# Moving the product for the maxima, the background slots and the first and last steps of a fused perceiver layer

## The chip, the core and the metric

One core of one Trainium2 chip runs the whole program. The time is device microseconds of one launch; a kernel's figure is the median of its runs. Engines are named as in the profile: PE (TensorE), DVE (VectorE), ACT (ScalarE), POOL (GpSimd), SP (the queue that issues most transfers).

## What is computed

x is (4, 256, 256), the context is (4, 4096, 256), all in float32. The reference applies three residual layers in turn:

```
x = x + cross_attention(layernorm(x), context)      # 8 heads of 64; keys and values of x and of the context joined: 4352 keys
x = routed(x)     # layernorm; a small network ranks the 256 tokens of a batch: the top 64 go through
                  # self-attention, the other 192 through a state-space scan (512 channels, 16 states)
x = x + experts(layernorm(x))    # router picks 2 of 8 experts per token: down(silu(gate(x)) * up(x))
```

## The kernel before

**Main loop.** The cross-attention is cut into 16 groups G (4 batches of 4 head pairs) and each group into 8 steps s, so n = 8G+s runs over N = 128 steps and two more. A step takes 32 queries of two heads against all keys. On PE it computes `scores(n)` into one PSUM area `su` (L1384, L1391). DVE copies `su` to SBUF and takes each row's maximum (`copy_max`, L1403, and the small `mq`, L1410). `stat(n)` is a product on PE that brings together the four partial maxima of a query (L1415, its result lies in `su` too); DVE reduces it to `nb` (L1420). ACT applies exponentials one step later (`exps(n-1)`, L1431), and DVE transposes the two heads (`turn(n-1, 0)`, `turn(n-1, 1)`, L1440). `scores(n+1)` overwrites `su`, so it waits for `nb`.

**Pieces.** The rest of PE's time in a step is filled with pieces of other work. In steps s=2, 3, 4 they are `v_chunk` (values of 512 context rows, L1368), nine per group; in s=6, 7, 0 `k_chunk` (keys for the next group, L1330, eight) and `k_self` (queries and own keys, L1341); in s=1 and 5, the value steps, four pieces of `values` (probabilities times values, L1449). `load_ctx` (L1235) brings each chunk's context tile on SP, in four buffers. In the first group step 1 has no piece, and in the last group steps 0, 6 and 7 have none.

**Sums.** At s=0, `sums(G-1)` forms reciprocals of the softmax sums; `spread` writes them to DRAM, `fetch` (L1486, on ACT's queue, at s=1) reads them back broadcast as `rs`, and `normalize` (L1502) multiplies each half of the output `ao` by them. `project` (L1506) and `add` put a finished batch into `x_sb`.

**Background.** Everything else of a batch runs as generators beside the main loop: `routed(b)` with router, self-attention, `ssm_front`, `ssm_scan`, `ssm_back`, then `sortable` and, for batch 2, `dispatch`, which sorts tokens of three batches by expert. Each generator yields (delay, share): it goes on no earlier than `now` plus delay, and only in a slot that has so much room left. `now` is a hand-written clock that the loop advances by estimated PE times; `slot(budget)` stands at fixed places of a step and lets each waiting generator take one stretch. So the order of instructions on every engine is fixed when the program is written, and each engine works its queue in order. In a scan stretch DVE runs one scan (L743) and POOL multiplies by `cb` (L749) and adds twice to `y` (L751); after two scans ACT makes new exponentials `da` (L731) and POOL new products `db` (L736). Each batch has 32 scans.

The fourth batch's background, the experts of the sorted tokens (19 blocks) and the dense experts of the last batch follow behind the main loop, once `dispatch` has set `ready`.

## Time and profile before

| | us |
|---|---|
| median of 3 runs | 1528.92 (1523.39 to 1531.32) |
| the profiled execution | 1526.89 |
| its span, first to last instruction | 1525.1 |
| main loop, from the first scores to the last ones' end | 24.9 to about 1242 |
| PE, DVE, ACT, POOL busy | 1444.4, 1061.7, 758.6, 404.5 |

A group's row gives an engine and a source line, the tiles it writes and reads, the count, the busy time and the mean in ns of one, then the engine's idle time ahead of these instructions and what ended it. A row of the waits gives who waited for whom: us in total, times, longest. A row in order of time gives start, duration, engine, line, and in brackets the idle time before it with its releaser. PE counts as busy while products overlap, so gaps show where it had nothing to do, not how fast it was.

### The profile page before, as it was taken

The page shows a single profiled execution, that of the slowest core. Times are in us where ns is not written, and L with a number is a line of the kernel's source. Part 1 is how long each engine was busy: PE and PEld are TensorE (multiplying, and loading weights), DVE is VectorE, ACT ScalarE, POOL GpSimd, SP SyncE. Part 2 cuts the span into 40 slices and gives each one's busy share as a digit, 9 for nine tenths or more (in the row PEclk, how much of TensorE's full clock was granted, in tenths as well). Part 3 has the DMA queues.
Part 4 walks back from the last instruction along what each step waited for, and adds up shares of the span by engine and source line. Part 5 has one row for each costly group of instructions (what it writes and reads, how often), then busy time and mean ns, then how long its engine had stood idle before and what let it go on. Part 6 is the DMA issues. An engine that isn't in the chain of part 4 may idle for free.

```text
span 1525.1 us, 35283 instructions
## 1 busy us (share of the span) xinstructions
PE 1444.4 (95%) x14630; PEld 1021.4 (67%) x14630; DVE 1061.7 (70%) x1824; ACT 758.6 (50%) x1484; POOL 404.5 (27%) x467
## 2 busy tenths in 40 slices
PE   7999999999999999999999999999998968898999
PEld 3747566677666566676757575767575657888887
DVE  1656665656698986666889956666989663699353
ACT  3444454454665645455766544556655522553311
POOL 1000000000078860000598800001989101111020
PEclk9999999999999999999999999999999979999999
DMA  6555534424445343425454444352543333787661
GB/s 230 156 148 150 162 117 155 156 88 138 136 132 173 122 136 128 157 78 154 145 151 145 147 142 132 105 164 87 191 138 107 105 125 114 218 274 232 222 198 53
DMA packets 160352, 225.42 MB, mean 148 GB/s; under 512 B 15520, under 2 KB 78752, under 8 KB 160192
## 3 DMA queue, kind: packets, MB, share of 16 engines
q1 hardware_dynamic: 149632, 208.96, 43.5%
q10 hardware_dynamic: 9072, 10.13, 2.0%
q0 software_dynamic: 1488, 4.07, 0.9%
q8 instruction: 116, 1.90, 0.5%
q14 instruction: 44, 0.36, 0.1%
HBM read 218.66 MB, written 4.46 MB: 146 GB/s over the span
## 4 chain that ended last, share of the span: by engine, by line
PE 60%; DVE 20%; POOL 9%; issue 5%; DMA 3%; ACT 2%; SPq 0%; ACTq 0%; DVEq 0%; POOLq 0%
PE psv L1368 10%; PE su L1384 10%; PE po L1449 10%; PE psk L1330 9%; DVE sp L1403 6%; DVE db L743 4%; POOL y L751 3%; POOL db L749 3%; POOL db L736 3%; DVE pt L1440 3%; PE su L1391 2%; PE pde L1906 2%; PE pg L1893 2%; PE pu L1893 2%; DVE db L839 2%
## 5 line engine op out<-in xcount | busy, mean ns | idle before, releaser
L1403 DVE TENSOR_SCALAR_CACHE_REDUCE sp<-su 128x1088 f32<-128x1088 f32 x256 | 318.8, 1282 | 186.8 <-PE su L1391 186.8
L1440 DVE STREAM_TRANSPOSE pt<-sp 128x1088 f32<-128x1088 f32 x256 | 327.5, 1293 | 30.6 <-PE po L1449 26.6
L1431 ACT ACTIVATE sp<-sp,nb 128x1088 f32<-128x1088 f32 x256 | 305.1, 1195 | 15.7 <-DVE nb L1420 13.8
L1449 PE MATMUL po<-pt,v 128*64 128x128 f32 x4352 | 261.0, 278 | 2.1 <-DVE pt L1440 1.3
L1384 PE MATMUL su<-kt,qh 64*32 64x512 f32 x4096 | 256.3, 610 | 4.5 <-DVE nb L1420 4.0
L1330 PE MATMUL psk<-ctx,wk 128*128 128x512 f32 x512 | 245.9, 614 | 11.7 <-DMA ctx<-in_ctxT 8.0
L1368 PE MATMUL psv<-wv,ctx 128*128 128x128 f32 x2048 | 252.3, 280 | 0.0
L1449 PEld LDWEIGHTS po<-pt,v 128*64 128x64 f32 x4352 | 242.4, 139 | 11.9 <-issue 6.3
L1368 PEld LDWEIGHTS psv<-wv,ctx 128*128 128x128 f32 x2048 | 237.7, 193 | 11.1 <-issue 8.9
L1330 PEld LDWEIGHTS psk<-ctx,wk 128*128 128x128 f32 x512 | 91.7, 192 | 100.3 <-issue 92.6
L1318 ACT COPY kt<-psk 128x512 f32<-128x512 f32 x128 | 74.6, 585 | 155.8 <-PE psk L1330 155.5
L1384 PEld LDWEIGHTS su<-kt,qh 64*32 64x32 f32 x4096 | 63.1, 108 | 124.0 <-issue 95.5
L1372 ACT COPY v<-psv 128x512 f32<-128x512 f32 x144 | 79.4, 558 | 134.1 <-PE psv L1368 132.8
L751 POOL TENSOR_TENSOR y<-y,db 128x192 f32<-128x192 f32 x192 | 139.7, 728 | 15.0
L743 DVE TENSOR_TENSOR_SCAN db<-da,db 128x384 f32<-128x384 f32 x96 | 126.4, 1317 | 11.4 <-POOL y L751 0.5
L749 POOL TENSOR_TENSOR db<-db,cb 128x384 f32<-128x384 f32 x96 | 108.1, 1126 | 43.6 <-DVE da L741 43.6
L395 POOL TENSOR_TENSOR kbd<-qk,hmask 128x512 f32<-128x512 f32 x8 | 8.6, 1096 | 403.1 <-ACT qk L385 403.1
L731 ACT ACTIVATE da<-delta,A_log_sb 128x192 f32<-128x192 f32 x192 | 75.4, 447 | 51.0 <-DVE da L741 31.5
L736 POOL TENSOR_TENSOR db<-bb,xc 128x384 f32<-128x384 f32 x96 | 99.5, 1059 | 0.2
L1391 PEld LDWEIGHTS su<-kx,qh 128*32 128x32 f32 x1024 | 20.2, 108 | 109.4 <-issue 109.4
L1415 PEld LDWEIGHTS su<-mq,same 128*128 128x128 f32 x256 | 40.8, 190 | 66.3 <-DVE mq L1410 46.9
L1496 ACT COPY ao<-po 128x128 f32<-128x128 f32 x32 | 8.4, 264 | 139.5 <-PE po L1449 139.5
(297 smaller groups left out, 1569.3 us busy)
## 6 DMA issues: line engine op xcount, KB each, us to landing
ctx<-in_ctxT SPq DMA_DIRECT2D x256, 512.0 KB
gateT<-in_gateT SPq DMA_DIRECT2D x27, 512.0 KB
upT<-in_upT SPq DMA_DIRECT2D x27, 512.0 KB
downT<-in_downT SPq DMA_DIRECT2D x27, 512.0 KB
bb<-bcd SPq DMA_DIRECT2D x24, 192.0 KB
cb<-bcd SPq DMA_DIRECT2D x24, 192.0 KB
wv<-in_wv SPq DMA_DIRECT2D x32, 128.0 KB
in_w<-in_in_w SPq DMA_DIRECT2D x32, 128.0 KB
```

The source lines that it names most:

```text
L736: nc.gpsimd.tensor_tensor(db, bbs[k], bc(xc[:, m, :], 1, SG), ALU.mult)
L743: nc.vector.tensor_tensor_scan(out=db, data0=da, data1=db, initial=0.0, op0=ALU.mult, op1=ALU.add,)
L749: nc.gpsimd.tensor_tensor(db, db, cbs[k], ALU.mult)
L751: nc.gpsimd.tensor_tensor(y[:, m, :], y[:, m, :], db[:, s, :], ALU.add)
L1330: nc.tensor.matmul(ps, wqk[G][:, 0, c, :], ct[:, c, :], start=(c == 0), stop=(c == KD - 1),)
L1368: nc.tensor.matmul(ps[:, i * P : (i + 1) * P], lhsT, wv[G][:, w, c, :], start=(c == 0), stop=(c == KD - 1),)
L1372: nc.scalar.copy(v.rearrange("p k d -> p (k d)"), ps[:, : n * P])
L1384: nc.tensor.matmul(su[q * 32 : (q + 1) * 32, SC[j] + lo : SC[j] + lo + 512], qT[r, s * 32 : (s + 1) * 32], kt[r, q, lo : lo + 512], start= ...
L1403: nc.vector.tensor_scalar(out=sps[n][j], in0=su[:, SU[j] : SU[j] + QK], scalar1=1.0, scalar2=None, op0=ALU.mult, op1=ALU.max, accum_out=nm ...
L1431: nc.scalar.activation(sps[n][j], sps[n][j], AF.Exp, bias=nbs[n][:, j : j + 1], accum_out=lss[b][:, hp, s, j : j + 1],)
L1440: nc.vector.transpose(pts[m, j][:, i, :], sps[n][j])
L1449: nc.tensor.matmul(pos[m][j * HD : (j + 1) * HD, :], vts[m // 2, k // 4][:, k % 4, j * HD : (j + 1) * HD], pts[m, j][:, :, kk * 32 : (kk + ...
```

## The change

In steps that aren't value steps, `stat` moves from ahead of the third piece into its middle (`mid`); in value steps it moves behind the third piece, and the first `normalize` follows it. A slot is added in value steps ahead of the first piece; in scan stretches some slots shrink to one scan, and a scan may follow after 1.9 instead of 2.2. Parts of `dispatch` may join in one slot (`fits`), and the last seven steps get larger slots (`more`). The first group's value chunks start in step 1, the last group's in its step 0, in a free key buffer. The late loads start at 70 instead of 15, and group 1's `wself` is loaded in step 6. The last batch's projection is done for three head pairs in step 126 and for the fourth at the end; a projection's two halves share one bank and are added together. In `ssm_back`, both products come ahead of both copies.

```diff
@@ -766,7 +766,7 @@
...
                     else:
-                        yield 2.2, 1.4
+                        yield 1.9, 1.4
@@ -873,6 +873,7 @@
                     ps[:n, q * D : (q + 1) * D], zs[:, m, q * P : q * P + n],
                     ow[m // 2][:, m % 2, :], start=(m == 0), stop=(m == NDT - 1),
                 )
+        for q, n in ((0, P), (1, NBOT - P)):
             nc.scalar.copy(dsort[:n, q, :], ps[:n, q * D : (q + 1) * D])
@@ -909,7 +911,10 @@
...
             yield 3.0, 0
+        if not late:
+            scanning.add(b)
         yield from st["late"] if late else ssm_scan(b, st)
+        scanning.discard(b)
@@ -1107,7 +1112,8 @@
...
-        yield 1.0, 1.25
+        if not fits(1.25):
+            yield 1.0, 1.25
         chosen(sl, slot)
@@ -1135,7 +1142,8 @@
...
         ats = []
         for i, tag in enumerate(("ua", "permT", "dsort")):
-            yield 1.0, 0.7
+            if not fits(0.7):
+                yield 1.0, 0.7
             at = bg.tile([P, 4, P], F32, tag=tag, name="at")
@@ -1173,6 +1181,13 @@
...
+
+    def fits(share):
+
+        if room[0] < share:
+            return False
+        room[0] -= share
+        return True
@@ -1253,13 +1268,14 @@
...
         def load_later():
 
-            yield 15.0, 0
+            yield 70.0, 0
             for b in range(1, B):
                 load_x(b)
                 yield 2.0, 0
             nc.sync.dma_start(out=wo, in_=a["xwo"].rearrange("(c p) m -> p c m", p=P))
             yield 2.0, 0
             yield from load_consts()
+            yield 10.0, 0
             start(routed(0))
@@ -1320,7 +1336,7 @@
...
-        def k_chunk(G, g):
+        def k_chunk(G, g, mid=None):
...
                     ps, wqk[G][:, 0, c, :], ct[:, c, :],
                     start=(c == 0), stop=(c == KD - 1),
                 )
+                if mid and c == 0:
+                    mid()
             keys_out(G, g * (CK // 4), ps)
@@ -1351,15 +1369,23 @@
...
-        def v_chunk(G, g):
+        def v_chunk(G, g, mid=None):
 
             b = G // NHP
             n = 4 if g < NCH else 2
-            v = wk.tile([P, n, P], F32, tag=f"v{n}", name="v", bufs=NCH if g < NCH else 1)
+            if G == NG - 1 and g < 3:
+
+                if g == 0:
+                    vts["first"] = wke.tile([P, 4, SQ], F32, tag="kt", name="vfirst")
+                v = vts["first"][:, g, : n * P].rearrange("p (k d) -> p k d", d=P)
+            else:
+                v = wk.tile([P, n, P], F32, tag=f"v{n}", name="v", bufs=NCH if g < NCH else 1)
             ps = ps_m.tile([P, 512], F32, tag="m", name="psv")
             if g < NCH:
                 ct = load_ctx(b, g)
             for i in range(n):
+                if mid and 2 * i == n - n % 4:
+                    mid()
@@ -1501,32 +1527,28 @@
...
+        def project(b, hps):
+
+            ps = bank("psx")
+            for half in range(2):
+                for hp in hps:
+                    nc.tensor.matmul(
+                        ps[:, half * D : (half + 1) * D],
+                        aos[b, hp][:, half * P : (half + 1) * P], wo[:, hp, :],
+                        start=(hp == hps[0]), stop=(hp == hps[-1]),
+                    )
+            return ps
+
+        def add(b, ps):
+            for half in range(2):
+                xb = x_sb[:, 2 * b + half, :]
+                nc.vector.tensor_tensor(xb, xb, ps[:, half * D : (half + 1) * D], ALU.add)
...
         def finish_batch(b):
 
             yield 1.0, 0.9
-            if b in psx:
-                ps, done_hp = psx[b], NHP - 1
-            else:
-                ps, done_hp = bank("psx"), 0
-                project(b, 0, ps, range(NHP))
-                add(b, 0, ps)
-            project(b, 1, ps, range(done_hp, NHP))
-            add(b, 1, ps)
+            add(b, project(b, range(NHP - 1 if b == B - 1 else 0, NHP)))
             finished.add(b)
@@ -1551,35 +1573,46 @@
...
-                if s % 4 == 1:
+                if G == 0 and s == 1:
+                    pieces = [lambda g=g: v_chunk(G, g) for g in range(2)]
+                elif s % 4 == 1:
                     m, took = n // 4 - 1, 1.95
-                    if m >= 0:
-                        pieces = [
-                            lambda i=i: values(m, i, min(i + 9, NJ)) for i in range(0, NJ, 9)
-                        ]
-                elif 2 <= s <= 4 and G < NG:
                     pieces = [
-                        lambda g=g: v_chunk(G, g) for g in range(3 * s - 6, 3 * s - 3)
+                        lambda i=i: values(m, i, min(i + 9, NJ)) for i in range(0, NJ, 9)
+                    ]
+                elif G < NG and (2 <= s <= 4 or s == 0 and G == NG - 1):
+                    at = {0: (2, 5, 7, 9), NG - 1: (3, 6, 8, 9)}.get(G, (0, 3, 6, 9))
+                    if s == 0:
+                        at = (0, at[0])
+                    else:
+                        at = at[s - 2 : s]
+                    pieces = [
+                        lambda mid=None, g=g: v_chunk(G, g, mid) for g in range(*at)
                     ]
                 elif G + 1 < NG:
                     if s == 0:
                         wqk[G + 1] = load_qk(G + 1)
+                    if s == (6 if G == 0 else 0):
                         wself[G + 1] = load_self(G + 1)
                     pieces = {
-                        0: [lambda g=g: k_chunk(G + 1, g) for g in range(3)],
-                        6: [lambda g=g: k_chunk(G + 1, g) for g in range(3, 6)],
+                        0: [lambda mid=None, g=g: k_chunk(G + 1, g, mid) for g in range(3)],
+                        6: [lambda mid=None, g=g: k_chunk(G + 1, g, mid) for g in range(3, 6)],
                         7: [lambda: k_self(G + 1)]
-                        + [lambda g=g: k_chunk(G + 1, g) for g in range(6, 8)],
+                        + [lambda mid=None, g=g: k_chunk(G + 1, g, mid) for g in range(6, 8)],
                     }[s]
...
-                def piece(i):
+                def piece(i, **mid):
                     if i < len(pieces):
-                        pieces[i]()
+                        pieces[i](**mid)
                     if i < len(pieces) or tail:
                         now[0] += took
+
+                def maxima():
+                    if new:
+                        stat(n)
@@ -1588,24 +1621,45 @@
...
                     copy_max(n)
+                if n == N - 2:
+
+                    part = project(B - 1, range(NHP - 1))
+                if tail:
+                    maxima()
+
+                more = 1.3 if n > N - 7 else 0.0
+                if s % 4 == 1 or more:
+                    slot(1.3 + more)
                 piece(0)
                 if s % 4 != 1:
-                    slot(1.3)
+                    slot(room[0] if more else 1.3)
                     piece(1)
                     if old:
                         turn(n - 1, 0)
-                    if new:
-                        stat(n)
-                        now[0] += 0.3
                     if s == 0 and n:
                         sums(G - 1)
                         now[0] += 0.2
+                    now[0] += 0.3
+                    slot(1.3 if tail else 0.5)
+                    if tail:
+                        piece(2)
+                    elif len(pieces) > 2:
+                        piece(2, mid=maxima)
+                    else:
+                        maxima()
                     if old:
                         turn(n - 1, 1)
-                    slot(1.3 if tail else 0.5)
-                    piece(2)
+                    if n == N - 2:
+                        add(B - 1, part)
                     if s == 0 and n:
                         spread(G - 1)
+                    slot(1.5 if scanning and s in ((4,) if n > N - 32 else (4, 7)) else 2.9 + more)
+                elif n == 1:
+                    piece(1)
+                    now[0] += 0.3
+                    turn(0, 0)
+                    maxima()
+                    turn(0, 1)
                     slot(2.9)
                 else:
                     last = s == 1 and G
@@ -1613,23 +1667,16 @@
                     if last:
                         fetch(G - 1)
                     piece(1)
-                    if new:
-                        stat(n)
-                        now[0] += 0.3
-                    slot(2.8)
+                    now[0] += 0.3
+                    slot((1.5 if scanning else 2.8) + more)
+                    piece(2)
+                    if not tail:
+                        maxima()
                     if last:
                         normalize(m - 1)
-                    if n == N + 1:
-
-                        psx[B - 1] = bank("psx")
-                        project(B - 1, 0, psx[B - 1], range(NHP))
-                        add(B - 1, 0, psx[B - 1])
-                        project(B - 1, 1, psx[B - 1], range(NHP - 1))
-                    piece(2)
                     slot(1.5)
                     piece(3)
-                    if n > 4:
-                        values_out(m)
+                    values_out(m)
                     if old:
                         turn(n - 1, 0)
                         turn(n - 1, 1)
```

More of the change, by code (lines that the diff above doesn't have):

```diff
@@ L889, in perceiver_layer @@
     done = set()
+    scanning = set()
     finished = set()
@@ L1125, in dispatch @@
         )
-        yield 1.0, 1.25
+        if not fits(1.25):
+            yield 1.0, 1.25
         inb = eq[:, : 2 * n * NB].rearrange(
@@ L1502, in normalize @@
             nc.vector.tensor_tensor(ao, ao, rss[G][:, q], ALU.mult)
-        def project(b, half, ps, hps):
-            for hp in hps:
-                nc.tensor.matmul(
-                    ps[:, half * D : (half + 1) * D],
-                    aos[b, hp][:, half * P : (half + 1) * P], wo[:, hp, :],
-                    start=(hp == 0), stop=(hp == NHP - 1),
-                )
-        def add(b, half, ps):
-            xb = x_sb[:, 2 * b + half, :]
-            nc.vector.tensor_tensor(xb, xb, ps[:, half * D : (half + 1) * D], ALU.add)
+        def project(b, hps):
[12 more added lines that the diff above has]
+                nc.vector.tensor_tensor(xb, xb, ps[:, half * D : (half + 1) * D], ALU.add)
         def finish_batch(b):
             yield 1.0, 0.9
-            if b in psx:
-                ps, done_hp = psx[b], NHP - 1
-            else:
-                ps, done_hp = bank("psx"), 0
-                project(b, 0, ps, range(NHP))
-                add(b, 0, ps)
-            project(b, 1, ps, range(done_hp, NHP))
-            add(b, 1, ps)
+            add(b, project(b, range(NHP - 1 if b == B - 1 else 0, NHP)))
             finished.add(b)
-        psx = {}
         with tc.manual_schedule():
```

## The prediction

> **What bounds the kernel now.** I read the shares of busy time first, then TensorE's waits, then stages and single steps.
>
> ```profile
> PE 1444.4 (95%) x14630; PEld 1021.4 (67%) x14630; DVE 1061.7 (70%) x1824; ACT 758.6 (50%) x1484; POOL 404.5 (27%) x467
> ```
> ```profile
> PE su L1415 <- DVE mq L1410: 27.4, 19, 3.4
> PE psk L1330 <- DMA ctx<-in_ctxT: 8.0, 3, 6.3
> PE psx L1506 <- DVE x_sb L1514: 1.9, 4, 0.6
> PE pssd L872 <- ACT dsort L876: 1.8, 4, 0.5
> ```
> TensorE is the bound of the whole. What it waits for is small and named: mostly the product for the maxima (L1415), which waits for VectorE. Next the stages (columns: PE, PEld, DVE, ACT, POOL busy with counts; clock; DMA share; GB/s): quiet, then scans, then the last steps.
>
> ```profile
> 250.00:300.00 50.00, 50.00 (x571) 33.82 (x565) 32.12 (x50) 24.20 (x44) 0.00 (x0) 1.00 0.41 133
> ...
> 450.00:500.00 50.00, 46.76 (x532) 30.51 (x517) 45.75 (x70) 30.44 (x65) 44.14 (x51) 1.00 0.49 154
> ...
> 1200.00:1250.00 50.00, 38.10 (x421) 26.67 (x420) 33.99 (x78) 20.22 (x35) 0.00 (x0) 0.85 0.26 82
> ```
> In quiet stages TensorE has no gap; in scan stages VectorE and GpSimd are nearly full as well. Measured from one step's scores to the next, the 14 scan steps of batch 0 (n=45 to 58, 431.1 to 566.4) last 135.3 us with 133.7 us of VectorE busy in them. So VectorE is the wall there. The step around its worst place, in order of time:
>
> ```profile
> 474.39 0.52 ACTq L1486 DMA_DIRECT2D rs<-rd  x1
> ```
> ```profile
> 478.79 0.99 DVE L1502 TENSOR_TENSOR ao<-ao,rs 128x128 f32<-128x128 f32 x1 [2.28 <-DMA rs<-rd]
> 479.70 2.49 DVE L1440 STREAM_TRANSPOSE pt<-sp 128x1088 f32<-128x1088 f32 x2
> ```
> ```profile
> 485.31 0.39 PE L1415 MATMUL su<-mq,same 128*128 128x8 f32 x2 [2.86 <-DVE mq L1410]
> ```
> The reciprocal sums are fetched on ACT's queue behind exponentials that wait for a scan, land 4.4 us later, and hold VectorE; one step on TensorE pays.
>
> **Moved maxima.** The loop to cover, in a quiet step:
>
> ```profile
> 603.32 0.28 PE L1415 MATMUL su<-mq,same 128*128 128x8 f32 x2
> ...
> 603.78 0.13 DVE L1420 TENSOR_REDUCE nb<-su 128x2 f32<-128x8 f32 x1
> ...
> 605.35 1.95 PE L1384 MATMUL su<-kt,qh 64*32 64x512 f32 x32
> ```
> In n=1 (product 41.93, next scores 42.57, nothing between) product, reduction and the next scores' start take 0.64 us. Behind the moved product half a chunk is left: 0.85 us (k chunk 3.70/2 us) or 0.94 (v chunk). So quiet steps stay as they are, and the product may come some 0.9 us later without a stall, in value steps 1.95 us (one piece more). Queued behind the reduction on VectorE are the second transposition and the next copies: the transposition ends at 605.1, the copies start at 607.73, so 0.9 us is free. The slot moved ahead of the product can put a table-waiting normalization before the reduction; no row shows that place. Bounds: 0, and one wait of 0.92 (psx L971 on ACT) in a few steps; I take 0.
>
> **First steps.** Weights wself for group 1 stand on SP before the first context tiles and wait for the queries (issued 24.42); the context goes out at 25.35 and TensorE waits 2.38:
>
> ```profile
> 29.55 5.37 PE L1330 MATMUL psk<-ctx,wk 128*128 128x512 f32 x8 [2.38 <-issue]
> ```
> Eight such products take 3.70 elsewhere, 5.37 here at half clock. Moved to step 6, that is gone: 2.38+1.67 = 4.0. n=1 now holds two v chunks (3.77), n=3 and n=4 lose them. A short step can't go under 6.7 us: scores 2.3, copies and mq 2.75, first transposition 1.3, reduction and signal 0.3. So n=1 to 4 go from 28.9 to 6.65+8.0+6.7+6.7 = 28.05: 0.9. The constants move from n=3..10 to n=9..16: SP's pile in front of n=8 (gaps 0.77 and 0.93) goes, with 0.6 at n=10 and 0.4 at n=16; each of the 17 loads still holds SP 0.4 to 2.4 us, among context tiles that run four ahead; cost 0, at worst the same 1.7 once more. Taken: 2.6. Together **-7.5**.
>
> **Projection and sort rows.** Both halves before one add: gaps 0.58, 0.52, 0.51 at n=34, 66, 98 go: **-1.6**. Both products before the two copies: 0.46 in each of four batches; three are in the sums below, the late one gives **-0.5**.
>
> **Scans.** Walking the slots: before 18 scans in 8 steps (2 in each plain step, 3 in each value step), after 16 (17 in the third batch), so 32 scans end at n=59, 91, 122 rather than 57, 89, 121. A scan costs VectorE
>
> ```profile
> L743 DVE TENSOR_TENSOR_SCAN db<-da,db 128x384 f32<-128x384 f32 x96 | 126.4, 1317 | 11.4 <-POOL y L751 0.5
> ```
> 1.32+0.06 us (with its memset, L741) and GpSimd 3.6 (1.06 L736, 1.13 L749, 2 x 0.73 L751): 16 in eight steps are 58 us of GpSimd in 67, which leaves it no bound, 18 were 65. The new slot ahead of the first value piece (1.3) is too small for a scan (1.4) and costs nothing there. Stalls in value steps and short ones of late copies vanish (n=53: 2.10; n=85: 1.67; n=55, 56 and others). But the slot order in the value step now puts one scan behind the normalization. At n=49 the odd scan, whose new exponentials block ACT, still stands before the fetch; VectorE comes to the sums earlier, waits until 478.8 all the same, then runs a scan (1.4), two transpositions, a normalization (0.3): copies at 484.0 instead of 482.4. TensorE, 0.4 earlier and with 0.95 more cover, stalls about 4.1 (was 2.86). At n=57 the walk has an odd scan before the fetch too, where before none was: 3.3 (was 0.89). In the third batch n=113 has an even one: its 2.86 mostly goes.
>
> Here the Trainium skill weighs in. The rows:
>
> ```profile
> 511.46 0.47 PE L1415 MATMUL su<-mq,same 128*128 128x8 f32 x2 [2.10 <-DVE da L741]
> 511.86 5.25 PE L1449 MATMUL po<-pt,v 128*64 128x128 f32 x64
> ```
> 64 products took 5.25 us after a gap of 2.10; they take 3.71 elsewhere. "TensorE: Matmul & The Clock Gate", in "Why this matters for your kernels", says that gaps up to about 3 us leave the clock alone. By the rule the removed 2.38, 2.10 and 1.67 return themselves only, and the sum is 1.7 to 5 us smaller; by the rows each returns 1.5 to 1.7 us more. I take the rows. Both agree against me on the stalls of 3 to 4 us that the change leaves: I charge one lost 1.7 in batches 0 and 1 each.
>
> Batch 0, n=45 to 62: 174.3 us, TensorE busy 164.4, less 1.7 of clock, plus 4.1+3.3+1.6 (transposes waiting for ACT, unchanged) +1.5 of small ones +1.7 clock = 174.8: **+0.5**. Batch 1: 176.5, busy 167.3, less 5.1, plus the same 12.2 = 174.4: **-2.1**. Third, n=109 to 119: two scans fewer, **-2.0**. If the fetch were no hindrance, each of the first two would return 7 to 8 more.
>
> **Last steps.** n=120 to 127 last 84.1 us with 16.5 us of gaps and VectorE busy 68.2. n=120 gets three v chunks: its 4.16 of gaps is filled, and n=123, 124 get short. (Its tiles reuse a key buffer last read in n=119; their context loads move up three places on SP, which runs ahead: 0.) But VectorE carries 9 scans there. By its queue n=120 takes 8.2, n=121 10.3 (TensorE's work); in n=121 the sums land at 20.5 us from n=120's start, then come a scan, transpositions (to 25.1), the copies of n=122 (28.0), the two last scans, which the larger slot puts ahead of the transposition, and the reduction at 32.4: 14.0 for n=122. n=123 takes 10.6 (scores 2.3, two chunks 3.8, the out-product 3.8, reduction), n=124 8.6, n=125 12.0 with its small products: 63.7 to the scores of n=126, instead of 65.4: -1.7. Dispatch comes a step earlier (tokens in n=127, not 128), its pieces fused in front of n=127's copies: 4.0 to the maxima of n=126, 2.8 for the counts, transposition 1.3, slots 1.6, transposition 1.3, partial add 0.8, the rest 3.5, copies to maxima 3.3: 18.6 instead of 15.1. Then tokens 3.3, transposition 1.3, weights 1.6, three transpositions with sums 4.2, values 8.1, and copy, normalization, one head pair's projection and add 2.0: 20.5 instead of 25.2, where TensorE stood at the sums (1263.15). Together **-2.9**, taken as 3. If VectorE falls behind further, this part costs 5; all gaps filled, it returns 12. The expert stage behind it moves as a whole.
>
> Sum: 7.5+1.6+0.5-0.5+2.1+2.0+3 = 16.2. The profiled execution took 1526.9 (span 1525.1), so 1510.7; it stood 2.0 under the median 1528.92, hence **1512**.
>
> **Rivals.** *The wall falls.* Sixteen scans in eight steps leave VectorE room: 8 x 5.6+16 x 1.38 = 67 us against TensorE's 67.6. If the sums land in time, 7.5 in each of two batches and 6 in the last steps come on top: 1512-21 = 1491. For it: VectorE's 98% share in scan steps; against: the fetch row. *Only covered time is removed.* VectorE remains the wall and the late end of the scans eats the last steps: -7.5-1.6 stays, +5 and +3 back: about 1527. *Slower: the maxima come too late.* In a step whose first transposition isn't done when the product lands, the next scores wait 0.64+1.29-0.85 = 1.08 us. It decides from 15 such steps on (16.2/1.08); in all 34 plain scan steps it would be 37, so 1512+37 = 1549. Against it: in quiet steps the first transposition ends at 603.85, some 0.35 us before the product would stand (604.2), and in scan steps TensorE already waits on VectorE. That the changed order isn't taken up is excluded: the order is written out by hand.
>
> **Numbers.** Forecast (1503 to 1521) 0.48; wall falls (1486 to 1503) 0.24; covered (1521 to 1537) 0.16; slower 0.12. About 0.5% is what a measurement of this kernel can tell from no change, so faster means under 1521.3: 0.72, within 0.16, slower 0.12. The range 1488 to 1532 leaves out the slower case, 0.05 of the covered one and 0.03 at the lower end: 0.20.
>
> **What would show it.** Right: no gap before n=0's second group of products and full clock there; L1415's 27.4 us halved; waits on psx L1506 and pssd L872 gone; n=50, 58, 82, 90 with gaps of 3 to 4 us behind DMA rs. Wrong: scores waiting for nb in quiet steps; scan steps at 8.0 us without gaps (the wall has fallen); the last 8 steps under 75 us.

## The result and the profile after

The changed kernel takes 1539.65 us in the median (1536.30 to 1546.39), the kernel before, on the same chip, 1526.95: **0.9% slower, ratio 1.0093 (95% interval 1.0074 to 1.0113)**. Forecast were 1512 and a gain of 16. The profiled execution took 1546.39 (span 1544.7), the slowest of the seven and 6.7 above their median; this matters in two rows below.

The page's busy time and TensorE's waits after:

```profile
PE 1451.4 (94%) x14630; PEld 1023.4 (66%) x14630; DVE 1059.1 (69%) x1826; ACT 757.3 (49%) x1484; POOL 391.1 (25%) x467
```
```profile
PE su L1441 <- DVE mq L1436: 23.6, 13, 8.4
PE psv L1394 <- ACT ao L1522: 12.4, 4, 4.9
PE psk L1346 <- DMA ctx<-in_ctxT: 11.4, 6, 6.1
...
PE po L1475 <- DVE pt L1466: 6.0, 2, 5.2
PE su L1441 <- DVE da L741: 4.8, 1, 4.8
```

The product for the maxima now stands at L1441. It waited for `mq` for 27.4 us in 19 places, now 23.6 in 13: fewer waits, but longer ones. One wait is new, values (psv) behind ScalarE's copy of the products (ao); another, the out-products (po) behind transpositions, has grown from 1.3 us in one place to 6.0 in two. The waits for the projection's bank and the sort rows are gone, as forecast. The same three stages as before (PE, PEld, DVE, ACT, POOL busy with counts; clock; DMA share; GB/s):

```profile
250.00:300.00 50.00, 50.00 (x531) 30.97 (x530) 32.15 (x51) 24.10 (x43) 0.00 (x0) 1.00 0.46 153
450.00:500.00 50.00, 42.98 (x475) 28.71 (x475) 37.20 (x60) 24.10 (x51) 31.43 (x38) 0.90 0.43 142
1200.00:1250.00 50.00, 37.67 (x400) 24.82 (x399) 31.43 (x59) 17.56 (x31) 7.54 (x10) 0.90 0.14 42
```

In the scan stage VectorE is busy 37.2 us of 50, not 45.8, and yet TensorE works less and its clock falls from 1.00 to 0.90. VectorE, nearly full there before, now stands waiting. By steps, measured from scores to scores in the two traces (us):

| steps | before | after | change | forecast |
|---|---|---|---|---|
| n=0 to 43 | 399.1 | 392.2 | -6.9 | -8.0 |
| 44 to 63 (batch 0 scans) | 189.2 | 197.8 | +8.6 | +0.5 |
| 64 to 75 | 126.3 | 128.1 | +1.8 | -0.5 |
| 76 to 95 (batch 1) | 191.4 | 197.3 | +5.9 | -2.1 |
| 96 to 107 | 126.2 | 126.4 | +0.2 | -0.5 |
| 108 to 119 (third batch) | 106.6 | 106.7 | +0.1 | -2.0 |
| 120 to 126 | 74.1 | 79.1 | +5.0 | -3.5 for both |
| 127 to the end | 287.3 | 291.4 | +4.1 | |

(The forecast's column sets its own terms into these rows; 0.8 more lies ahead of the first scores.) Two of these rows probably hold most of the 6.7 us by which this execution was slow: row 64 to 75, with a wait of 2.26 us for a context tile at n=64, and the last row, which takes 286 to 290 in most of the variants below that keep the new pace. What remains to be explained are the two scan rows, which lose 14.5 where a gain of 1.6 was forecast, and n=120 to 126.

Four steps make up 13.4 us of the scan rows' loss: n=50 takes 17.6 us (before 11.1), n=58 14.2 (13.3), n=82 17.6 (12.0), n=90 13.7 (13.3). The others nearly cancel: n=53 and 85 lose their stalls (14.1 and 13.7, now 10.3), and side work that comes later makes n=61 and 93 longer (12.0 and 12.9, now 16.5). n=49 and 50, in order of time, first SP's and ScalarE's queues, then VectorE, then TensorE:

```profile
465.83 0.32 SPq L714 DMA_DIRECT2D bb<-bcd  x1
466.24 2.20 SPq L1250 DMA_DIRECT2D ctx<-in_ctxT  x4
```
```profile
467.69 0.52 ACTq L1512 DMA_DIRECT2D rs<-rd  x1
...
479.59 0.80 ACT L731 ACTIVATE da<-delta,A_log_sb 128x192 f32<-128x192 f32 x2 [9.92 <-DVE db L743]
480.30 0.24 ACT L1522 COPY ao<-po 128x128 f32<-128x128 f32 x1
```
```profile
478.12 0.29 DVE L1528 TENSOR_TENSOR ao<-ao,rs 128x128 f32<-128x128 f32 x1 [9.29 <-DMA rs<-rd]
...
478.54 0.96 DVE L743 TENSOR_TENSOR_SCAN db<-da,db 128x384 f32<-128x384 f32 x1
...
484.52 0.17 DVE L1436 TENSOR_TENSOR mq<-nm,quarter 128x8 f32<-128x8 f32 x1
```
```profile
480.59 2.08 PE L1394 MATMUL psv<-wv,ctx 128*128 128x128 f32 x8 [4.94 <-ACT ao L1522]
484.74 0.59 PE L1441 MATMUL su<-mq,same 128*128 128x8 f32 x2 [2.07 <-DVE mq L1436]
```

Read it from the top. SP stood before a load of `bb` until 465.83, then sent four context loads in one go (two more at 473.9 and 475.7). Before, three such loads went out 9.8 us ahead of the fetch, not next to it:

```profile
464.60 1.41 SPq L1235 DMA_DIRECT2D ctx<-in_ctxT  x3
```

Now the small fetch of the reciprocal sums, issued 1.45 us behind the first of the four, landed after 10.4 us instead of 4.4. VectorE idled 9.3 us. Behind its normalization came a scan, behind the scan ScalarE's exponentials, behind these ScalarE's copy `ao`, and that copy held the PSUM bank for the next values. TensorE lost 7.0 us, and ran at half clock behind it (granted clock 0.50; eight psv products take 2.08, elsewhere 1.14).

### The profile page after: what moved, and what is told of

Its sections match the earlier page's. It is cut to its first block, busy times and chain, and to the rows that moved or that the text cites. A ratio compares the mean times of both kernels' runs of the same rounds, so it can differ in the third digit from the quotient of the medians.

```text
span 1544.7 us, 35273 instructions
## 1 busy us (share of the span) xinstructions
PE 1451.4 (94%) x14630; PEld 1023.4 (66%) x14630; DVE 1059.1 (69%) x1826; ACT 757.3 (49%) x1484; POOL 391.1 (25%) x467
## 4 chain that ended last, share of the span: by engine, by line
PE 69%; DVE 20%; DMA 6%; issue 2%; ACT 2%; SPq 1%; POOL 0%; ACTq 0%; DVEq 0%
PE su L1410 12%; PE po L1475 12%; PE psv L1394 12%; PE psk L1346 10%; DVE sp L1429 5%; DVE db L743 4%; DVE pt L1466 3%; DMA rs<-rd 3%; DMA ctx<-in_ctxT 3%; PE su L1417 2%; PE pde L1953 2%; PE pu L1940 2%; PE pg L1940 2%; DVE db L839 2%; PE psks L1359 1%
## 5 line engine op out<-in xcount | busy, mean ns | idle before, releaser
L1394 PE MATMUL psv<-wv,ctx 128*128 128x128 f32 x2048 | 258.8, 283 | 12.4 <-ACT ao L1522 12.4
L1410 PE MATMUL su<-kt,qh 64*32 64x512 f32 x4096 | 261.4, 619 | 8.1 <-DVE nb L1446 6.8
L1346 PE MATMUL psk<-ctx,wk 128*128 128x512 f32 x512 | 249.2, 615 | 12.6 <-DMA ctx<-in_ctxT 11.4
L1394 PEld LDWEIGHTS psv<-wv,ctx 128*128 128x128 f32 x2048 | 241.8, 195 | 25.0 <-ACT ao L1522 13.1
L1475 PE MATMUL po<-pt,v 128*64 128x128 f32 x4256 | 250.6, 274 | 0.0
L1475 PEld LDWEIGHTS po<-pt,v 128*64 128x64 f32 x4256 | 234.0, 137 | 9.0 <-issue 6.4
L743 DVE TENSOR_TENSOR_SCAN db<-da,db 128x384 f32<-128x384 f32 x96 | 125.0, 1302 | 11.0
L749 POOL TENSOR_TENSOR db<-db,cb 128x384 f32<-128x384 f32 x96 | 97.2, 1012 | 119.3 <-DVE da L741 90.2
L1446 DVE TENSOR_REDUCE nb<-su 128x2 f32<-128x8 f32 x128 | 20.1, 157 | 134.8 <-PE su L1441 134.7
L1417 PEld LDWEIGHTS su<-kx,qh 128*32 128x32 f32 x1024 | 20.2, 108 | 111.6 <-issue 111.6
L1441 PEld LDWEIGHTS su<-mq,same 128*128 128x128 f32 x256 | 42.6, 193 | 59.6 <-DVE mq L1436 29.9
```

What stands on the lines that cost most here:

```text
L743: nc.vector.tensor_tensor_scan(out=db, data0=da, data1=db, initial=0.0, op0=ALU.mult, op1=ALU.add,)
L749: nc.gpsimd.tensor_tensor(db, db, cbs[k], ALU.mult)
L1346: nc.tensor.matmul(ps, wqk[G][:, 0, c, :], ct[:, c, :], start=(c == 0), stop=(c == KD - 1),)
L1394: nc.tensor.matmul(ps[:, i * P : (i + 1) * P], lhsT, wv[G][:, w, c, :], start=(c == 0), stop=(c == KD - 1),)
L1410: nc.tensor.matmul(su[q * 32 : (q + 1) * 32, SC[j] + lo : SC[j] + lo + 512], qT[r, s * 32 : (s + 1) * 32], kt[r, q, lo : lo + 512], start= ...
L1475: nc.tensor.matmul(pos[m][j * HD : (j + 1) * HD, :], vts[m // 2, k // 4][:, k % 4, j * HD : (j + 1) * HD], pts[m, j][:, :, kk * 32 : (kk + ...
```

## The experiments

Theory A, **late sums**: a later or slower fetch of `rs` is the common cause of n=50, 58, 82, 90. Theory B, **order**: the product for the maxima, moved behind the third piece, or the normalization behind it, costs directly. Beside these stood the last steps. All ratios are to the kernel before on the same chip.

**Pace undone (u_pace).** The pauses and slots of the scans as before, all else changed:

```diff
-  yield 1.9, 1.4
+  yield 2.2, 1.4
...
-  slot(1.5 if scanning and s in ((4,) if n > N - 32 else (4, 7)) else 2.9 + more)
+  slot(2.9 + more)
...
-  slot((1.5 if scanning else 2.8) + more)
+  slot(2.8 + more)
```

> The changed kernel with the old pacing of the scans alone put back (2.2 instead of 1.9; no slot cut to 1.5). Theory A (late sums): with fewer scans per step the load of bb and cb waits longer on SP, the context tiles behind it go out in one burst, the fetch of rs shares the 16 transfer engines with that burst (10.4 us instead of 4.4) and holds DVE, then ACT and a PSUM bank. Then the old pacing gives back 10 to 16 us, about 1526, and the gaps of 7.0 and 4.5 at n=50, 58, 82, 90 fall under 3. Theory B (order in the value step): the scan and the maxima behind the third piece are at fault, whatever the pace; then this run stays within 5 us of 1540.

**Order undone (u_order).** The maxima ahead of the third piece again, the first normalization ahead of the third piece. Shown is the half for the value steps; in the other steps the product stands ahead of the sums again:

```diff
   piece(1)
+  if not tail:
+      maxima()
   slot((1.5 if scanning else 2.8) + more)
+  if last:
+      normalize(m - 1)
   piece(2)
-  if not tail:
-      maxima()
-  if last:
-      normalize(m - 1)
...
```

> The changed kernel with the product for the maxima back ahead of the third piece, and the first normalization back ahead of the value step's third piece. Theory A: the late sums stay, so 1540 to 1550 (short stalls of the maxima come back). Theory B: 10 us or more are given back, 1530 or less.

**Last steps undone (u_last).** The last group's chunks in their old steps, `more = 0.0`, `fits` always false.

> The changed kernel with the last group's value chunks back in steps 122 to 124 (own buffers), no larger slots in the last seven steps and dispatch in its old pieces. Theory A with a second cause: the last steps cost 9 to 10 us (5 to n=127, 4 behind it; the late expert weights wait for the key buffer that now holds values), so about 1530. Rival: DVE is the wall there and order is indifferent: within 3 us of 1540.

**Fetch first (fetch).** The changed kernel with one line moved:

```diff
+  if last:
+      fetch(G - 1)
   slot(1.5)
-  if last:
-      fetch(G - 1)
   piece(1)
```

> The changed kernel with the fetch of rs ahead of the slot of the second piece, so ahead of the exponentials on ACT that wait for a scan. Theory A: it goes out some 3.6 us earlier (464 instead of 467.7 in batch 0), ahead of the context burst at 466.2, lands within 5 us, and the gaps at n=50, 58, 82, 90 go: 15 to 22 us back, about 1520. Rival: the transfer engines are full anyway or DVE is the wall: under 6 us back.

| kernel | median | ratio (interval) | n=44 to 63 | 76 to 95 | 120 to the end |
|---|---|---|---|---|---|
| changed | 1539.65 | 1.0093 (1.0074 to 1.0113) | 197.8 | 197.3 | 370.5 |
| u_pace | 1514.75 | 0.9937 (0.9914 to 0.9961) | 191.8 | 191.8 | 353.7 |
| u_order | 1540.44 | 1.0096 (1.0073 to 1.0119) | 201.5 | 199.9 | 361.9 |
| u_last | 1532.49 | 1.0046 (1.0028 to 1.0064) | 197.9 | 196.9 | 364.2 |
| fetch | 1508.57 | 0.9892 (0.9868 to 0.9916) | 184.1 | 184.1 | 363.8 |

Undoing the order changes nothing in total, and the scan rows become 3.7 and 2.6 us longer, so B falls as the cause of their loss. The zero is a balance, though: from n=120 on u_order is 8.6 us shorter than the changed kernel's slow execution, and 5.0 shorter than u_first (below), which has the same last steps. One line moved returns 31 us and makes the kernel 1.1% faster than before; both pace and fetch return more than expected. In the fetch's kernel VectorE at n=49 has no idle time before the normalization, and n=50 has a gap of 0.24 at the maxima:

```profile
467.19 0.56 DVE L1528 TENSOR_TENSOR ao<-ao,rs 128x128 f32<-128x128 f32 x1
```
```profile
475.79 0.39 PE L1441 MATMUL su<-mq,same 128*128 128x8 f32 x2 [0.24 <-DVE mq L1436]
```

But an earlier fetch cures two things at once: a late place in ScalarE's queue, and a slow transfer. Read from the trace's DMA packets, n=49 (issue counted from the step's first scores; packets from the issue):

| kernel | issue | first packet | last packet |
|---|---|---|---|
| before | +8.7 | 1.3 | 4.1 |
| changed | +8.4 | 5.3 | 9.8 |
| u_pace | +9.2 | 1.3 | 4.1 |
| fetch | +1.8 | 1.3 | 4.1 |

At n=49 the issue is no later than before. Only the transfer is slower. (At n=57 both move: issue from +3.9 to +8.4, last packet from 4.0 to 5.7.) The stretch from the issue to the normalization, before and after, with the DMA engines' share and GB/s at the end of the row:

```profile
474.39:478.79 4.40, 4.40 (x79) 2.64 (x76) 2.01 (x3) 3.60 (x10) 4.16 (x6) 1.00 0.17 44
```
```profile
467.69:478.12 10.43, 7.96 (x102) 5.99 (x102) 1.13 (x3) 1.52 (x4) 7.60 (x10) 1.00 0.87 283
```

The fetch met engines that were busy 87%, with the four context loads ahead of it above all. Next, a kernel that takes the burst away and leaves the fetch where it is.

**bb and cb on GpSimd's queue (pool_loads).** SP then no longer waits for `bb` and `cb` ahead of the context loads:

```diff
-  nc.sync.dma_start(
+  nc.gpsimd.dma_start(
       out=t, in_=st["bcd"][o, SG * k : SG * (k + 1), :].partition_broadcast(P)
```

> The changed kernel with the loads of bb and cb (L714) issued on GpSimd's queue in place of SP's; the fetch of the reciprocal sums stays where it is. This takes away what holds SP, so that the context loads no longer go out in a burst just ahead of the fetch. Late sums by a collision: in the changed kernel the fetch of n=49 is issued 8.4 us into the step, as before, but its first packet runs 5.3 us after the issue and its last 9.8 (before 1.3 and 4.1), with 2.95 MB moved in the 11 us around it; now the last packet should run some 4 to 5 us after the issue, n=50 and 82 go from 17.6 to 11 to 13 us, n=58 and 90 from 14.2 to 12 to 13, and the time to 1520 to 1530, if the issues cost GpSimd little. Late sums by the place in ACT's queue alone: the normalization stands as late as now (18.8 us into n=49), and the time stays at 1538 to 1542. If the time stays though the fetch lands early, GpSimd's own cost for the issues took the gain.

1527.30, ratio 1.0013 (0.9999 to 1.0027): 12 us returned. The issue is at +8.6, so as late as ever, and the last packet runs 4.1 us after it; n=50 and 82 take 11.7. The stretch, the normalization and the maxima of n=50:

```profile
467.08:471.54 4.46, 4.46 (x74) 2.68 (x74) 1.55 (x3) 1.52 (x4) 4.15 (x6) 1.00 0.10 33
```
```profile
471.54 0.55 DVE L1528 TENSOR_TENSOR ao<-ao,rs 128x128 f32<-128x128 f32 x1 [2.90 <-DMA rs<-rd]
```
```profile
479.23 0.39 PE L1441 MATMUL su<-mq,same 128*128 128x8 f32 x2 [3.21 <-DVE mq L1436]
```

The collision is shown, apart from the place in the queue. The 3.2 us that stay (at n=50 and at n=58) are the stalls that the prediction had put at 4.1 and 3.3: the fetch behind a scan's exponentials. GpSimd paid 27 us for 48 issues and waited 19.1 us for the loads themselves, which it does not in the changed kernel (13.1 for cb, 6.0 for bb).

**The bank (vout).** Is the held PSUM bank a cost of its own? The last slot of a value step moved behind the copy `ao`, the transpositions and the second normalization:

```diff
-  slot(1.5)
   piece(3)
   values_out(m)
...
   if last:
       normalize(m)
+  slot(1.5)
+  if last:
```

> The changed kernel with the last slot of each value step moved behind the step's copy of the products, transpositions and second normalization. ScalarE then copies the products out (ao, L1522) ahead of the exponentials that wait for the scan, so the PSUM bank comes free early and TensorE's wait of 4.94 us (psv behind ao) at n=50 goes; the fetch stays as late as it is. If the bank is a cost of its own: n=50 and 82 go from 17.6 to about 13, and the time to 1527 to 1533. If VectorE's late sums alone set the step, the same idle time shows up as a wait for mq (2.1 us before it, 6 to 7 then), n=50 and 82 stay at 16.5 to 17.6, and the time at 1535 to 1541.

1550.65, ratio 1.0174 (1.0148 to 1.0200), slower than either expectation. The wait for the bank is gone, and its time is found whole at the maxima of n=50, which takes 18.3:

```profile
484.60 0.60 PE L1441 MATMUL su<-mq,same 128*128 128x8 f32 x2 [8.55 <-DVE mq L1436]
```

The bank was only the first to wait on a late VectorE. Why the kernel lost 11 us on top (n=82 went from 17.6 to 20.2, where the last packet came 11.7 us after the issue) was not followed further.

**First steps undone (u_first).** Load times, `wself` and the first chunks as before:

```diff
-  yield 70.0, 0
+  yield 15.0, 0
...
-  if G == 0 and s == 1:
-      pieces = [lambda g=g: v_chunk(G, g) for g in range(2)]
...
-  if s == (6 if G == 0 else 0):
+  if s == 0:
```

> The changed kernel with its first steps undone: self weights of group 1 loaded in step 0, one v chunk's worth less in n=1, the constants from n=3 on. By the measured stretch (n=0 to 7: 66.8 before, 61.1 after) it should be 5 to 6 us slower than the changed kernel, 1544 to 1547, with n=0 to 7 at 66 to 67. Rival: the gain is given back at n=16, where the changed kernel waits 1.9 us for a context tile that before it did not; then the difference is 3 to 4 us.

1548.84, ratio 1.0142 (1.0113 to 1.0171), so the first steps return 7 to 9 us, more than expected; n=0 to 7 last 69.0, not 61.0. Some 1.6 us of this is no part of the kernel before: n=2 takes 9.6 here, in both other kernels 8.0. The gap at n=16 is 1.9 in the changed profile and 0.3 here.

**Fetch first in the kernel before (b_fetch).** The same line moved, nothing else.

> The kernel before with one edit, the fetch ahead of the slot of n=8k+1. Late sums limit the kernel before too, in small: its stalls at n=50, 82 and 114 (2.9 us each with 1.5 of half clock behind them) and n=58, 90 (1.4) shrink, 1512 to 1520. Rival: VectorE is its wall there (133.7 of 135.3 us), a fetch earlier only moves the wait, 1522 to 1526.

1518.19, ratio 0.9960 (0.9945 to 0.9975). The same delay was in the kernel before, in small: n=50, 82 and 114 fall from 11.1, 12.0 and 12.1 to 9.8, 9.6 and 9.8.

**Fetch and old pace (fetch_pace).**

> The changed kernel with the fetch ahead of the slot of n=8k+1 and the old pace of the scans. Late sums as the common cause: each of the two alone gave back 31 and 25 us, mostly at the same steps (n=50, 58, 82, 90), so together they give little more than one, 1500 to 1510; what the old pace adds is the last stretch (from n=127 on 277 in place of 288) and what it takes is VectorE as the wall in the scan steps (n=44 to 63 at 186 to 190 in place of 184). If they were independent, 1540 - 56 = 1484.

1511.13, ratio 0.9906 (0.9881 to 0.9931), just above the range expected: together no more than the fetch alone. The scan rows go to 191.1 (the old pace puts more scans into each step again), while n=120 to the end falls to 350.9. So the new pace pays in batches 0 and 1 and costs at the end.

**Old pace in the third batch only (fetch_pace3).**

```diff
-  yield 1.9, 1.4
+  yield (2.2 if b == B - 2 else 1.9), 1.4
...
-  slot(1.5 if scanning and s in ((4,) if n > N - 32 else (4, 7)) else 2.9 + more)
+  slot(1.5 if scanning and n < N - 32 and s in (4, 7) else 2.9 + more)
...
-  slot((1.5 if scanning else 2.8) + more)
+  slot((1.5 if scanning and n < N - 32 else 2.8) + more)
```

> The changed kernel with the fetch ahead of the slot of n=8k+1, and the old pace of the scans in the third batch only (n from 96 on). If the new pace is what costs time in the last steps (scans that end in n=122 rather than 121 push dispatch behind n=127's scores): the stretch from n=120 to the end goes from 363.8 us to 351 to 355, the scan steps of batches 0 and 1 stay at 184 for twenty steps, and the time is 1494 to 1500, the fastest so far. If the last stretch of the two kernels with the old pace is short for another reason (the place of the side work that comes down from batches 0 and 1), it stays at 362 to 365 and the time at 1505 to 1510.

**1498.68, ratio 0.9836 (0.9811 to 0.9861), the lowest ratio here, faster than both kernels** (fetch_nomore and fetch_pace3_last, below, can't be told from it). The scan rows stay at 184, n=120 to the end takes 351.2. The last steps with the fetch alone, then with the old pace: the maxima of n=122 and the scores of n=123, the third batch's last scan, dispatch's tokens.

```profile
1170.17 0.39 PE L1441 MATMUL su<-mq,same 128*128 128x8 f32 x2 [1.45 <-DVE da L741]
...
1174.08 3.67 PE L1410 MATMUL su<-kt,qh 64*32 64x512 f32 x32 [2.53 <-DVE nb L1446]
```
```profile
1171.70 1.07 DVE L743 TENSOR_TENSOR_SCAN db<-da,db 128x384 f32<-128x384 f32 x1
...
1237.21 0.18 DVE L1160 CAST tokens<-pstok 128x19 int32<-128x19 f32 x1 [4.97 <-PE pstok L1156]
```
```profile
1163.55 1.07 DVE L743 TENSOR_TENSOR_SCAN db<-da,db 128x384 f32<-128x384 f32 x1
...
1218.99 0.18 DVE L1160 CAST tokens<-pstok 128x19 int32<-128x19 f32 x1 [1.93 <-PE pstok L1156]
```

With the new pace the last scan runs 9.9 us into n=122; with the old one it ends before n=122 begins (1164.74), and the scores of n=123 don't wait. Tokens come 18 us after n=127's first scores (1219.1) in the one, at them (1218.9) in the other.

**With GpSimd's loads as well (best).**

> The fetch ahead of the slot, the old pace in the third batch, and the loads of bb and cb on GpSimd's queue. With the fetch early the burst of context loads hurts nobody: the same as without the third edit, 1493 to 1501. If the burst still delays context tiles (n=64: 2.3 us of waiting in the changed kernel), 2 to 4 us faster than that; if the issues cost GpSimd more than they save, 2 to 6 slower.

1508.00, ratio 0.9902 (0.9877 to 0.9926): 9 us slower than without them, more than expected. With the fetch early there is no collision left to cure. The third batch's steps n=108 to 119 go from 106.8 to 113.4, those from n=120 on from 351.2 to 354.2, while the scan rows of batches 0 and 1 lose nothing (182.7 and 183.8, without these loads 184.1 and 184.2).

**Which of the last steps' edits.** All with the fetch first. fetch_last undoes all three, as u_last did:

> The changed kernel with the fetch ahead of the slot and the last steps undone (the last group's chunks back in their steps, no larger slots, every item of dispatch in its own slot). If the last steps' change returns what the prediction gave it (3 us), this is slower than the fetch alone: 1510 to 1514. If it costs, as the loss of 7 us without the fetch suggests, 1501 to 1506. In between, the 7 us came from the collision at n=121 and 122 (16.0 us against 11.6) and the change itself is worth nothing.

fetch_nofits undoes the joining of dispatch's items:

```diff
-  if room[0] < share:
-      return False
...
+  return False
```

> The changed kernel with the fetch ahead of the slot and no fusing of dispatch's items in one slot (every item its own). As the prediction had it, fusing brings dispatch's tokens a slot earlier: without it they come later behind n=127's scores and the time is 1510 to 1514. If what costs the last steps is the fused run of items ahead of n=127's copies (TensorE waits 7.7 us for them), 1503 to 1506.

fetch_nomore undoes the larger slots:

```diff
-  more = 1.3 if n > N - 7 else 0.0
+  more = 0.0
```

> The changed kernel with the fetch ahead of the slot and no larger slots in the last seven steps. If the larger slots cost, by putting two scans ahead of the transposition of n=122 (gap 1.5 at the maxima and 2.5 at its end, then half clock), n=122 goes from 12.3 to 8 to 9 and the time to 1503 to 1507. If they pay, by bringing dispatch forward, 1510 to 1516.

fetch_novlast undoes the moved chunks:

```diff
-  if G == NG - 1 and g < 3:
+  if False:
...
-  elif G < NG and (2 <= s <= 4 or s == 0 and G == NG - 1):
-      at = {0: (2, 5, 7, 9), NG - 1: (3, 6, 8, 9)}.get(G, (0, 3, 6, 9))
+  elif G < NG and 2 <= s <= 4:
+      at = {0: (2, 5, 7, 9)}.get(G, (0, 3, 6, 9))
```

> The changed kernel with the fetch ahead of the slot and the last group's v chunks back in n=122 to 124. n=120 then has gaps of 4 to 5 us again, n=122 to 124 are fuller. If moving them up pays as the prediction had it (they fill gaps of 4.2 us), 1510 to 1513; if the gap only moved to n=122 and 124, 1506 to 1510; if TensorE's filled n=120 is no gain and the short n=124 to 126 are a loss, 1503 to 1506.

fetch_pace3_last undoes all three and has the old pace in the third batch:

> The fetch ahead of the slot, the old pace in the third batch, and all three edits of the last steps undone. If the edits cost whatever the pace is, the 5 us come on top of the old pace's 10: 1492 to 1496. If they cost only with the late scans, they pay 0 to 4 here: 1498 to 1503.

| kernel | median | ratio (interval) | n=120 to 126 | 127 to the end |
|---|---|---|---|---|
| fetch | 1508.57 | 0.9892 (0.9868 to 0.9916) | 76.3 | 287.5 |
| fetch_last | 1503.76 | 0.9867 (0.9843 to 0.9891) | 71.2 | 290.0 |
| fetch_nofits | 1507.25 | 0.9886 (0.9858 to 0.9915) | 76.4 | 283.9 |
| fetch_nomore | 1501.77 | 0.9844 (0.9817 to 0.9870) | 65.2 | 292.3 |
| fetch_novlast | 1507.70 | 0.9887 (0.9860 to 0.9914) | 78.1 | 286.0 |
| fetch_pace3_last | 1501.97 | 0.9842 (0.9815 to 0.9868) | 72.8 | 283.4 |

The larger slots cost about 7 us; the moved chunks and the fused items can't be told from nothing. Without larger slots the steps n=120 to 126 are 11.1 us shorter: n=122 takes 9.7 in place of 12.3, since the last two scans no longer stand between n=122's copies and its reduction, n=123 8.1 in place of 12.7, n=125 12.4 in place of 16.4. Behind n=127 they lose 4.8 of it again. fetch_nomore returned more than expected; fetch_nofits fell between its two expectations. With the old pace there are no such scans left, and all three edits together are worth nothing measurable (0.9842 against 0.9836).

## Why the prediction was wrong

**First steps: right.** Forecast -7.5, measured -6.9 with 0.9 from the projection in it (n=34), and 7 to 9 by u_first. n=0 went from 11.92 to 7.81, 4.1 us against 4.0 worked out; its products run at full clock:

```profile
27.92 4.56 PE L1346 MATMUL psk<-ctx,wk 128*128 128x512 f32 x10
```

n=1 to 4 went from 28.94 to 27.35. The worst case named for the late loads, 1.7 us lost once more, appeared in this profile as 1.9 at n=16.

**Projection and sort rows: right.** The gaps are gone, and n=34, 66 and 98 take 11.5 us in place of 12.3.

**Moved maxima: the 0 holds as a balance.** u_order finds 0 in total, made up of a gain in the scan rows and a loss in the last steps; no run undoes the order with the fetch early. The rival "maxima come too late" gave 1549 and lay nearest in time, but by a mechanism that did not occur: from n=6 to n=122 no scores wait for nb by more than 0.25 us.

**Scans, batches 0 and 1: wrong, +14.5 in place of -1.6.** The step that failed is "VectorE comes to the sums earlier, waits until 478.8 all the same". It kept the fetch's 4.4 us as a constant of the transfer. In all sixteen fetches in the trace of before the last packet comes 4.0 to 5.3 us after the issue, so nothing in it spoke against that; but the prediction had moved scans, and with them the loads of bb and cb that hold SP, without asking what SP would send once it was released. The stalls of 4.1 and 3.3 were right as far as they went: without the collision both measure 3.2. With it they are 7.0 and 4.5. pool_loads puts the collision at 12 us (11.6 of it in these two rows), and GpSimd's issues are paid out of that. A second term of the sum was too small as well, the clock, charged with one lost 1.7 in each batch: in n=44 to 63 TensorE is busy 184.1 us where the same products take 178.6 in the fetch's kernel, whose granted clock stays at 1.00 there, so the clock costs 5.5 us (batch 1: 183.6 and 178.3). Without the collision the two rows still stand at +2.5 and +0.4, not +0.5 and -2.1. That is mostly the clock again: TensorE is busy 182.9 and 182.0 us in them, 4.3 and 3.7 more than in the fetch's kernel, where 1.7 each had been charged.

One reading under it was wrong as well. The 133.7 us of VectorE in n=45 to 58 come near the sum of its instructions' durations (133.2), which overlap; the profile's busy time is 124.4 of 135.3, a share of 92% and not 98%:

```profile
431.10:566.40 135.30, 126.97 (x1429) 81.76 (x1433) 124.38 (x192) 77.81 (x157) 112.09 (x127) 0.99 0.49 154
```

**If the fetch were no hindrance: nearly right.** The prediction said that batches 0 and 1 would each return 7 to 8 more than its sum; with the fetch first they measure -5.1 and -7.3 against before, where -7 and -9.6 would follow. The fetch, named against "the wall falls", was the right obstacle. VectorE's share is no lower then (115.8 of 125.0 us in n=45 to 58, 93%), but TensorE idles only 5.5 us in n=44 to 63, before 9.9.

**Third batch: -2.0 forecast, +0.1 measured.** n=114 is shorter, as forecast (10.4 us, before 12.1), but the fetch met traffic here too (last packet 5.2 us after the issue, before 4.3), and n=112, 115 and 116 are 3.1 longer together. With the burst away (pool_loads) these steps take 105.2, so -1.4.

**Last steps: wrong.** To the scores of n=126 the sum was 63.7; it measures 71.4 (before 65.4). The terms: n=122 16.0 (14.0), n=123 11.8 (10.6), n=125 16.4 (12.0). The walk had the two last scans ahead of n=122's transposition, but took the steps behind it at TensorE's own work at full clock. In the trace the maxima of n=122 wait 4.82 us, and the scores of n=123 and of n=125 start behind a wait for nb; both sets of scores run at half clock:

```profile
1204.99 0.39 PE L1441 MATMUL su<-mq,same 128*128 128x8 f32 x2 [4.82 <-DVE da L741]
...
1209.22 3.48 PE L1410 MATMUL su<-kt,qh 64*32 64x512 f32 x32 [2.21 <-DVE nb L1446]
```
```profile
1229.19 3.51 PE L1410 MATMUL su<-kt,qh 64*32 64x512 f32 x32 [2.66 <-DVE nb L1446]
```

For n=122 the sums were in part at fault: the walk had them at 20.5 us from n=120's start, and n=121's normalization begins at 22.5, because its fetch was issued 9.2 us into the step (before: 3.1). With the fetch first n=122 takes 12.3. For n=123 and 125 the larger slots were: without them these steps take 8.1 and 12.4.

"Dispatch comes a step earlier" failed too: tokens come 18.1 us after n=127's first scores, before 14.4. The cause is the pace: scans that end a step later push dispatch back more than the larger slots and fused items bring it forward. fetch_pace3 shows it: from n=127 on 276.9 us in place of 287.5, and 2.0 less ahead of it.

**The clock rule.** The prediction weighed the Trainium skill's "TensorE: Matmul & The Clock Gate", section "Why this matters for your kernels", by which gaps up to about 3 us leave the clock alone, against the rows, and took the rows. Its rows hold: the granted clock fell to 0.50 for 3.41 us at the gaps of 2.38, 2.10 and 1.67 us in the kernel before, and after the gap of 2.66 at n=125 above; by the rule that step would be 1.5 us shorter. (At n=123 the clock had been at half since 1205.55, behind the 4.82.) But a gap's length alone does not decide. The same 2.66 us at n=125 of the fetch's kernel left the clock at 1.00:

```profile
1195.02 1.95 PE L1410 MATMUL su<-kt,qh 64*32 64x512 f32 x32 [2.66 <-DVE nb L1446]
```

The granted clock's own records tell the two apart. In each of the 18 traces all its changes stand on one grid of 3.41 us. In the changed kernel the 2.66 us lay inside one stretch of this grid (1226.03 to 1229.44), in the fetch's kernel it was split, 0.73 and 1.93 us, between two.

## What to carry to other kernels

A transfer's latency read from one trace belongs to the traffic that ran beside it: when a change moves what holds a queue, work out what that queue releases at once, and which small, urgent transfer lies in its way. Issue a small transfer that a whole chain waits for as early as its data are there; here one moved line returned 31 us in the changed kernel and 6 in the kernel before. A looser pace that frees an engine in the middle can push the last dependent work past the end, so the last batch may want a tighter one.

## What the hardware showed that was not expected

- A fetch of 128 KB whose last packet comes after 4.1 us when the DMA engines are 0.10 to 0.17 busy had its first packet after 5.3 us and its last after 9.8 when four loads of 512 KB had been issued on another queue from 1.45 us before it to just behind it (0.87 of the DMA engines busy, 283 GB/s). That transfers of different queues share the same 16 engines is what the Trainium skill says ("DMA: Bandwidth & Descriptors", "Issuing engines are not separate DMA queues"); what it costs a small one is this run's number.
- The clock goes by how long TensorE is idle within a fixed stretch, not by a gap's length. In the 18 traces, cut into stretches of 3.41 us on each one's grid, every stretch at full clock in which TensorE was idle for 2.02 us or more was followed by half clock (105 of 105). Below 1.55 us it was 8 of 3805; between these, 26 of 50. So two gaps of 3.21 us in pool_loads can differ. At n=50 the clock fell 1.54 us behind the gap's end, at 480.77; eight products still ran at full clock (1.14 us), then the scores took 3.52:

```profile
480.54 3.52 PE L1410 MATMUL su<-kt,qh 64*32 64x512 f32 x32
```

At n=58 it fell at 552.45, 1.4 us before the gap's end, and the eight products ran at half clock (2.05 us). The Trainium skill's "TensorE: Matmul & The Clock Gate", under "What's actually happening", describes such a free-running window of about 3.4 us; the threshold within it is these traces' own.
- 48 direct loads issued by GpSimd took it 0.56 us each (27 us in all). In the kernel with the lowest ratio the same loads cost 9 us of time, 6.6 of them in the third batch, whose old pace puts 18 scans into eight steps, and none in batches 0 and 1 with 16. GpSimd also waits there for the loads (24.7 us for cb, 6.0 for bb), which it does not when SP issues them. Which of the two costs the time is open.
